# The inverse transform's second and third width groups, one row later each, in a fused window-attention and Fourier kernel

## The chip, the core and the metric

The kernel runs on one core of a Trainium2 chip. The core has a matrix engine (PE, with its own unit PEld for loading weights), a vector engine (DVE), an activation engine (ACT), a general engine (POOL) and a queue engine (SP) that issues nearly all DMAs. Each takes its instructions in order; they wait for each other through semaphores. The metric is the device time of one execution in microseconds, as the median of several runs: 3237.37 us before the change (three runs, 3235.12 to 3238.8). All arithmetic is in float32.

## What is computed

The input is 32 images of 56 x 56 tokens with 128 channels. Two residual layers follow each other, and each normalises its input over groups of 4 channels first:

```python
x = x + window_attention(group_norm(x))   # windows of 7 x 7, shifted by 3, 4 heads, relative bias, mask
x = x + feedforward(fourier(group_norm(x)))
def fourier(x):                            # for the width and for the height
    modes = dct(x)[..., :32]               # first 32 modes along that axis
    mixed = einsum('bixy,ioy->boxy', modes, w)   # a 128 x 128 matrix for each mode
    return idct(mixed, zero beyond mode 32)      # summed over both axes
def feedforward(h):
    return relu(h @ W1 + b1) @ W2 + b2     # 128 -> 512 -> 128
```

The part that the change touches is the last step of `fourier` for the width axis: the inverse transform from 32 modes back to 56 columns, which is added onto what the height axis left.

## The kernel before

The work is cut into *cycles*. In cycle r the attention works on one row of windows (7 token rows): image r // 8, attention row i = r % 8. The Fourier layer and the feed-forward of an image run behind its attention; the helper `fourier(cycle)` gives, for every cycle, the one or two images that are in that phase and their step c. An image passes steps c = 0 to 15, so two images overlap: steps c and c + 8 always share a cycle. With the attention rows they stand like this:

| attention row i | 3 | 4 | 5 | 6 | 7 | 0 | 1 | 2 |
|---|---|---|---|---|---|---|---|---|
| younger image, step c | 0 | 1 | 2 | 3 | 4 | 5 | 6 | 7 |
| older image, step c | 8 | 9 | 10 | 11 | 12 | 13 | 14 | 15 |

Below a cycle is called by its steps: "the row of 2/10" is the cycle in which one image is at step 2 and the one before it at step 10. Eight cycles, one period, take about 97 us, and 31 such periods follow each other. When the attention of the last image is over, a shorter loop body works off the rest (the tail: step 0 of the last image and everything behind it).

What the steps do, as far as the change and the prediction speak of it:

- Forward transform (`transform`, L756) for the width at step 0 and for the height at steps 1 and 2. DVE transposes the result out of a PSUM bank (`turn_modes`, L771, called from `columns_turn` at steps 1 and 2), ACT scales it (`scale_modes`, L778) and adds the mean's part (`shift_modes`, L783) into the tile `y`.
- Mixing (`mix`, L803, copied by ACT at L811): height groups at step 3, width groups at steps 4 and 5. The result `z` goes through DRAM (`zscr`) and comes back turned as the tile `zT` (`load_modes`, L824), of which there are two buffers.
- Inverse transform (`modes_back`, L842, then `fetch_back`). Each axis has four groups of 16, 16, 16 and 8 lines. A group of 16 lines is 16 matmul instructions (each is two passes, so the profile counts 32) into two banks. For the height ACT copies the banks into the tile `xf` (L865). For the width DVE adds them onto `xf` (L860), 2 instructions of 128 x 448. Which group is done at which step is told by `back_groups(c)`.
- Feed-forward at steps 8, 9, 10, 12, 13, 14 and 15 (`FF_AT`; step 11 has none): `ff_in` (L885, printed as L124, the helper `halved`) reads 512 tokens of `xf`, ACT applies bias and ReLU (L887), `ff_out` (L124 and L920) makes the output, POOL adds the second bias to the residual (L892) and DVE adds both (L930). Group 0 of `ff_in` needs the first width group, group 1 (step 9) the second, group 3 (step 12) the third, group 5 (step 14) the fourth.

In a cycle PE's order is: q and k (L124 into `pa`), `ff_in`, the attention-value product of an earlier row (L592, inside `eighths`, with `transform` behind it), the scores (L498) and the inverse transform (both in `quarters`: the scores first where the row has a feed-forward, the inverse transform first where it has none), v (L476), the mixing, `ff_out`, the projection (L637). Where the row has no feed-forward, two mixes come ahead of `eighths` and two behind v.

DVE's order in a cycle: tokens of the next image, `turn_modes` or the bank readers of `eighths` (L622), the scores' bias (L506, two), the row maximum (L516), further `turn_modes`, `last_fetch` (L860 for the steps above 8), the transpose of the probabilities (L575), the sums (L528), the reciprocal (L530), and the adds at L930 and L645. POOL subtracts the maximum (L517) and ACT takes the exponential (L523).

PSUM has eight banks: four `pa` for attention, four `pc` for the rest, each set handed out in turn. A matmul into a bank waits until its last reader is done. The order on PE, DVE, ACT and POOL is the program's; SP's is chosen by the scheduler, which issues a load as soon as its buffer can be free.

Of the kernel before, what the change touches and what calls it, by code (L numbers as in the profile page):

```python
# [50 lines left out]
def swin_fourier_kernel(  # L51
# [75 lines left out]
    def load_tokens(im, i):  # L127

        n0, n1 = WS * i // 2, WS * (i + 1) // 2
        t = xr_sb[i % 2]  # L130
        for a, e, p, src in chunks_of(x, im.b, n0, n1):
            nc.sync.dma_start(t[p, a - n0 : e - n0], src)
        im.xr[i] = t
# [11 lines left out]
    def load_quarter(b, k, u):  # L145

        if b > 1:
            t = work.tile([P, HW, KB], F32, tag="xin", name="xin", bufs=1)
        else:
            t = y_of[k][:, : S * KB].rearrange("p (w c) -> p w c", w=S)  # L150
            t = t[:, u * HW : (u + 1) * HW]
        rows = slice(k * (S - KB), k * (S - KB) + KB)
        for cb in range(C // KB):
            cs = slice(cb * KB, (cb + 1) * KB)
            queue = nc.scalar if b == 0 and cb % 2 else nc.sync
            queue.dma_start(t[cs], x[b, rows, u * HW : (u + 1) * HW, cs])
        return t
# [111 lines left out]
    def mix_weights(k):  # L269
        dst, src = ((w1sb, w1), (w0sb, w0))[k // 4]  # L270
        m = slice(k % 4 * NM // 4, (k % 4 + 1) * NM // 4)
        nc.sync.dma_start(dst[:, m], src[:, m])
# [58 lines left out]
    def image_begin(b):  # L331
        im = Image()
        im.b = b
        im.half, im.xw, im.xr, im.eT = {}, {}, {}, {}
        return im
# [3 lines left out]
    def turn_quarter(im, k, u):  # L339

        slot = WS * ROWS[k]
        if u == 0:
            im.half[k] = big.tile(
                [P, NWR * WS * ROWS[1] + JP - WT], F32, tag="xw", name="xw", bufs=3
            )
            nc.vector.memset(im.half[k][:, NWR * slot : NWR * slot + JP - WT], 0.0)
        slots = im.half[k][:, : NWR * slot].rearrange("p (j h s) -> p s j h", j=NWR, s=WS)
        slots = slots[:, :, :, :KB]
        xin = xins.pop((im.b, k, u)).rearrange("p (m s) c -> p s m c", s=WS)
        m0, m1 = u * NP, (u + 1) * NP  # L350
        nc.vector.transpose(slots[:, : WS - SS, m0:m1], xin[:, SS:])
        if u == 0:
            nc.vector.transpose(slots[:, WS - SS :, NWR - 1], xin[:, :SS, 0])
            nc.vector.transpose(slots[:, WS - SS :, : NP - 1], xin[:, :SS, 1:])
        else:
            nc.vector.transpose(slots[:, WS - SS :, m0 - 1 : m1 - 1], xin[:, :SS])
        im.first = (SS * WS, WS * WS)
        windows = im.half[k][:, : NWR * slot].rearrange("p (j t) -> p j t", j=NWR)
        for i in range(NP):
            t0 = im.first[k] + i * WT  # L360
            im.xw[NP * k + i] = windows[:, :, t0 : t0 + WT]

    def copy_wrap(im, copy):
        a, b = (
            t[:, : NWR * WS * n].rearrange("p (j h s) -> p j h s", j=NWR, s=WS)
            for t, n in zip((im.half[0], im.half[1]), ROWS)
        )
        copy(b[:, :, KB:], a[:, :, :SS])

    def row_stats(im, i):  # L370
        if i == 0:
            im.st = small.tile([P, NWR, 6], F32, tag="st0", name="st0", bufs=2)
        nc.vector.bn_stats(im.st[:, i], im.xw[i])
# [392 lines left out]
    def turn_modes(im, width, h, r):  # L766

        p = im.py[width, h][r]
        t = work.tile([P, 4, C], F32, tag="z", name="modes", bufs=4)
        t = t.rearrange("p k c -> p (k c)")[:, : 2 * CH * KB]  # L770
        nc.vector.transpose(t, p[:, : 2 * CH * KB])  # L771
        im.modes.setdefault((width, h), []).append(t)
# [78 lines left out]
    def fetch_back(im, width, g):  # L851

        l0, n = LINES[g]
        nch = n // 4
        px = im.px.pop((width, g))
        for li in range(2):
            src = px[li][:, : nch * 2 * S]
            if width:
                dst = im.xf[:, l0 : l0 + n].rearrange("p (c l r) w -> p l c (r w)", l=2, r=2)
                nc.vector.tensor_tensor(  # L860
                    dst[:, li], src.rearrange("p (c m) -> p c m", c=nch), dst[:, li], ALU.add
                )
            else:
                dst = im.xf[:, :, l0 : l0 + n].rearrange("p h (c l r) -> p l c h r", l=2, r=2)
                nc.scalar.copy(dst[:, li], src.rearrange("p (c h r) -> p c h r", c=nch, r=2))  # L865
# [98 lines left out]
    def row(r):  # L964
        return (images[r // NWR], r % NWR) if 0 <= r < NB * NWR else (None, 0)

    def fourier(cycle):

        b, c = divmod(cycle - CONV_BEGIN, NWR)
        return [(images[b - k], c + k * NWR) for k in (1, 0) if 0 <= b - k < NB]  # L970

    def back_groups(c):

        if c in (5, 6, 7):
            return [(c == 7, (c + 1) % 2 * 2 + j) for j in range(2)]
        return [(True, c // 2 - 3)] if c in (10, 12) else []

    def load_back(cycle):
        for im, c in fourier(cycle):
# [134 lines left out]

    def last_fetch(cycle):
        for im, c in fourier(cycle):
            if c > 8:
                for width, g in back_groups(c):
                    fetch_back(im, width, g)

    def columns_turn(cycle, r):
        for im, c in fourier(cycle):
            if c in (1, 2):
                turn_modes(im, False, c - 1, r)
# [154 lines left out]
    with tc.manual_schedule(engines={ET.PE, ET.Activation, ET.DVE, ET.Pool}):  # L1279
        with tc.manual_schedule(engines={ET.SP}):  # L1280
            images[0] = image_begin(0)
            for k in range(2):
                for u in range(2):
                    turn_quarter(images[0], k, u)
                if k:
                    copy_wrap(images[0], nc.vector.tensor_copy)
                for u in range(2):
                    xins[1, k, u] = load_quarter(1, k, u)
                for i in range(NP * k, NP * k + NP):
                    row_stats(images[0], i)  # L1290
            for i in range(2):
                load_tokens(images[0], i)
            for m in range(8):
                mix_weights(m)
            for _ in range(3):
                norm_step(-1)
            for r, t in ((0, 0), (0, 1), (1, 0)):
                for half in range(2):
                    bias_and_mask(nc.vector, r, t, half)
            extra = big.tile([P, S, S], F32, tag="xf", name="a_extra", bufs=2)  # L1300
            extra = extra.rearrange("p r w -> p (r w)")[:, : AT + JP - WT]
            nc.gpsimd.memset(extra[:, AT:], 0.0)
            a_ends.append(extra)
            a_sb.append(extra[:, :AT].rearrange("p (t w j) -> p t w j", t=NH, w=NP))
            for cycle in range(CONV_BEGIN):
                first_rows(cycle)
        for cycle in range(CONV_BEGIN, NB * NWR + CONV_BEGIN + FF_AT[-1] - NWR + 1):
            halves_first(cycle)
            if not row(cycle - 3)[0]:
                eighths(cycle)  # L1310
                for r in range(2):
                    columns_turn(cycle, r)
                behind_max(cycle)
                half_columns(cycle)
                half_columns(cycle, True)
                scale_first(cycle, 0)
                scale_first(cycle, 1)
                load_first(cycle)
                last_out(cycle)
                quarters(cycle)  # L1320
                last_fetch(cycle)
                load_back(cycle + 1)
                continue
            if not has_ff(cycle):
                half_columns(cycle)
            eighths(cycle)
            early = any(c == 10 for _, c in fourier(cycle))
            if early:
                columns_turn(cycle, 0)
            quarters(cycle)  # L1330
            if row(cycle)[0]:
                attn_max(cycle)
            if not early:
                columns_turn(cycle, 0)
            columns_turn(cycle, 1)
            last_fetch(cycle)
            if row(cycle)[0] and cycle % NWR in LATE_SQUARES:
                sum_squares(*row(cycle - 4))
                next_tokens(cycle)
            behind_max(cycle)  # L1340
            load_first(cycle)
            halves_last(cycle)
# [62 lines left out]
```

## Time and profile before

| what | value |
|---|---|
| median of three runs | 3237.37 us (3235.12 to 3238.8) |
| the profiled execution's own time | 3239.0 us |
| its span, first to last instruction | 3236.4 us |
| mean granted PE clock | 0.993 |
| one period of 8 cycles, mean of 22 in the middle | 97.1 us |
| its rows, i = 0 to 7 | 15.65, 10.09, 10.12, 13.39, 12.68, 13.20, 8.28, 13.67 us |
| PE busy, first 150 us | 93.97 us |
| PE busy, 600 to 3000 us | 597 to 598 of each 600 us |
| PE busy, the last 107 us | 98.64 us |

The profiled execution stands 1.6 us above the median of the runs. Its span is 2.6 us shorter than its own time. A timeline line reads: start, duration, engine, line, operation, out<-in, shape and count, and in brackets the engine's idle time ahead of it and what ended that. A matmul's end is modelled, so what PE does is best read from the starts.

### The profile page before, as it was taken

What the parts mean: (1) busy time and instruction counts of PE and PEld (TensorE: products, weight loads), DVE (VectorE), ACT (ScalarE), POOL (GpSimd) and SP (SyncE); (2) the same over time, 40 slices, a digit from 0 to 9 for tenths busy, and PEclk for the clock granted to TensorE, in tenths of its full rate; (3) what the DMA queues carried; (4) which work ended last, traced back from release to release, by engine and by line L of the source; (5) the groups of instructions that cost most, each with busy time, mean ns of one, the idle gap of its engine ahead of it and who ended that gap; (6) DMA issues with size and microseconds to landing.
All of it is one profiled execution on the core that took longest, in us unless ns stands there. A gap on an engine that the chain in (4) does not pass through costs nothing.

```text
span 3236.4 us, 151985 instructions
## 1 busy us (share of the span) xinstructions
PE 3148.4 (97%) x65664; PEld 2348.9 (73%) x65664; DVE 2516.3 (78%) x4751; ACT 2183.5 (67%) x4004; POOL 2294.3 (71%) x2570
## 2 busy tenths in 40 slices
PE   5789999999999999999999999999999999999999
PEld 4567777777777777777777777777777777777776
DVE  7678888888888888887888888878888888888741
ACT  4566776666776676776676777666776666776663
POOL 5467777777777777777777777777777777777741
PEclk9899999999999999999999999999999999999999
DMA  6446566655556665556666656556666556665453
GB/s 128 98 118 147 139 139 148 138 147 147 139 137 148 138 148 144 140 138 147 138 147 145 141 138 147 138 142 150 141 139 146 138 144 148 141 140 142 117 145 89
DMA packets 1171652, 448.47 MB, mean 139 GB/s; under 512 B 527690, under 2 KB 1141116, under 8 KB 1170980
## 3 DMA queue, kind: packets, MB, share of 16 engines
q1 hardware_dynamic: 1162788, 437.41, 57.0%
q8 instruction: 514, 8.42, 1.2%
q10 hardware_dynamic: 7584, 1.18, 0.3%
q14 instruction: 158, 1.29, 0.1%
q0 software_dynamic: 608, 0.17, 0.0%
HBM read 277.00 MB, written 161.48 MB: 135 GB/s over the span
## 4 chain that ended last, share of the span: by engine, by line
PE 50%; DMA 0%; issue 0%; ACT 0%; DVE 0%; SPq 0%; DVEq 0%; ACTq 0%
PE pc L124 23%; PE pa L124 5%; PE pa L476 4%; PE pc L803 4%; PE pa L498 3%; PE pa L637 3%; PE pa L592 3%; PE pc L842 3%; PE pc L756 2%; PE pc L920 0%; DMA zT<-zscr 0%; ACT hid L887 0%; PE pa L703 0%; DMA out_dram<-res 0%; ACT xf L865 0%
## 5 line engine op out<-in xcount | busy, mean ns | idle before, releaser
L547 POOL TENSOR_TENSOR blocks<-a,rs 32x272 f32<-32x272 f32 (+3 forms) x1434 | 1217.4, 856 | 389.2 <-DVE rs L530 271.6
L124 PE MATMUL pc<-wff,hid 128*64 128x128 f32 x12288 | 714.0, 273 | 2.4 <-ACT hid L887 1.2
L124 PE MATMUL pc<-xf,wff 128*64 128x512 f32 (+2 forms) x3584 | 714.1, 539 | 1.3 <-DVE xf L860 1.3
L124 PEld LDWEIGHTS pc<-wff,hid 128*64 128x64 f32 x12288 | 680.0, 137 | 12.2 <-ACT hid L887 6.0
L517 POOL TENSOR_TENSOR a<-a,mx 128x784 f32<-128x784 f32 x250 | 376.3, 1505 | 297.7 <-DVE mx L516 270.8
L124 PEld LDWEIGHTS pc<-xf,wff 128*64 128x64 f32 x3584 | 263.1, 136 | 372.5 <-issue 292.7
L887 ACT ACTIVATE hid<-pc,b1sb 128x512 f32<-128x512 f32 (+2 forms) x896 | 499.8, 641 | 41.6 <-PE pc L124 41.0
L124 PE MATMUL pa<-xw,wn 128*64 128x392 f32 x2048 | 393.1, 499 | 28.6 <-ACT wn L429 27.9
L506 DVE TENSOR_TENSOR a<-pa,bm 128x392 f32<-128x392 f32 x500 | 259.0, 560 | 166.0 <-PE pa L498 153.7
L483 ACT COPY v<-pa 128x512 f32<-128x512 f32 x256 | 151.9, 593 | 286.0 <-PE pa L476 283.4
L463 ACT ACTIVATE k<-pa,bqkv,heads 128x392 f32<-128x392 f32 x512 | 318.5, 673 | 15.5 <-ACT q L450 1.1
L138 POOL TENSOR_TENSOR xr<-xr,bproj 128x384 f32<-128x384 f32 (+1 forms) x256 | 292.4, 1142 | 44.7 <-DMA xr<-in_x_dram 22.4
L892 POOL TENSOR_TENSOR res<-res,b2sb 128x512 f32<-128x512 f32 (+1 forms) x224 | 251.7, 1124 | 87.4 <-DMA res<-scr 70.0
L778 ACT ACTIVATE y<-modes,rstd 128x448 f32<-128x448 f32 x256 | 276.8, 1140 | 42.4 <-DVE modes L771 31.8
L450 ACT ACTIVATE q<-pa,bqkv 128x392 f32<-128x392 f32 x256 | 149.6, 585 | 227.5 <-PE pa L124 225.6
L523 ACT ACTIVATE a<-a 128x784 f32<-128x784 f32 x250 | 214.0, 856 | 130.9 <-POOL a L517 130.5
L575 DVE STREAM_TRANSPOSE eT<-blocks 128x1024 f32<-128x1024 f32 x240 | 295.3, 1230 | 0.0
L592 PEld LDWEIGHTS pa<-eT,v 49*32 49x32 f32 x16384 | 173.0, 106 | 158.7 <-issue 69.7
L476 PE MATMUL pa<-wn,xw 128*64 128x128 f32 x4096 | 281.5, 279 | 1.6 <-issue 1.2
L528 DVE TENSOR_REDUCE sm<-a 128x16 f32<-128x784 f32 x250 | 239.9, 959 | 53.5 <-ACT a L523 53.4
L516 DVE TENSOR_REDUCE mx<-a 128x16 f32<-128x784 f32 x250 | 242.2, 969 | 7.6
L476 PEld LDWEIGHTS pa<-wn,xw 128*64 128x64 f32 x4096 | 219.7, 137 | 36.5 <-issue 2.4
(126 smaller groups left out, 4980.4 us busy)
## 6 DMA issues: line engine op xcount, KB each, us to landing
zscr<-z SPq DMA_DIRECT2D x512, 112.0 KB
xin<-in_x_dram SPq DMA_DIRECT2D x480, 112.0 KB
htok<-scr SPq DMA_DIRECT2D x128, 392.0 KB
zT<-zscr SPq DMA_DIRECT2D x192, 256.0 KB
res<-scr SPq DMA_DIRECT2D x160, 256.0 KB
out_dram<-res SPq DMA_DIRECT2D x160, 256.0 KB
scr<-x SPq DMA_DIRECT2D x256, 112.0 KB
xr<-in_x_dram SPq DMA_DIRECT2D x256, 84.0 KB
```

The source lines that it names most:

```text
L124: nc.tensor.matmul(dst[ps], lhsT=lhsT[:, ps], rhs=rhs, start=start, stop=stop)
L138: nc.gpsimd.tensor_tensor(piece, piece, bproj.unsqueeze(1).to_broadcast([P, n, C]), ALU.add)
L463: nc.scalar.activation(k_sb[:, u], pk[:, :RT].rearrange("p (w j) -> p w j", j=WT), AF.Identity, bias=im.bias[:, 3 + u : 4 + u], scale=head ...
L476: nc.tensor.matmul(pv[HALVES[w % 2], w // 2 * C : (w // 2 + 1) * C], lhsT=im.half[i // NP][:, t0 : t0 + JP], rhs=im.w[:, 2 * C : 3 * C], s ...
L506: nc.vector.tensor_tensor(a[:, 2 * hp : 2 * hp + 2, :, 0:WT].rearrange("p u w j -> p w u j"), ps[hp][:, :RT].rearrange("p (w u j) -> p w u ...
L517: nc.gpsimd.tensor_tensor(a3, a3, mx.unsqueeze(2).to_broadcast([P, 2 * NWR, WT]), ALU.subtract)
L547: nc.gpsimd.tensor_tensor(dst[to, k, :, :n], a3[src, :, kb * KB : kb * KB + n], rs[src].unsqueeze(2).to_broadcast([src.stop - src.start, 2 ...
L575: nc.vector.transpose(eT.rearrange("p t (k j) -> p k t j", k=2), blocks[r % 2])
L592: nc.tensor.matmul(po4[u][h * HD : (h + 1) * HD, pr], lhsT=v[ks, pr, h * HD : (h + 1) * HD], rhs=eT[ks, h * NP + pr, :WT], start=True, sto ...
L778: nc.scalar.mul(y[:, r], t.rearrange("p (n k) -> p n k", k=NM), im.rstd)
L887: nc.scalar.activation(hf[:, :n], ph[:, :n], AF.Relu, bias=b1sb[:, f : f + 1])
L892: nc.gpsimd.tensor_tensor(im.res[:, :k], im.res[:, :k], b2sb.unsqueeze(1).to_broadcast([P, k, C]), ALU.add,)
```

## The change

The first width group stays at step 7 and the fourth at step 12. The second moves from step 7 to step 8, the third from step 10 to step 11. `last_fetch`, which adds a width group behind the row maximum, now takes step 8 in as well. The special order of the row of 2/10, in which the first `turn_modes` of step 2 stood ahead of the scores, is gone: both `turn_modes` of that row now come behind the row maximum.

```diff
     def back_groups(c):
-        if c in (5, 6, 7):
-            return [(c == 7, (c + 1) % 2 * 2 + j) for j in range(2)]
-        return [(True, c // 2 - 3)] if c in (10, 12) else []
+        if c in (5, 6):
+            return [(False, 2 * (c - 5) + j) for j in range(2)]
+        width_at = (7, 8, 11, 12)
+        return [(True, width_at.index(c))] if c in width_at else []
...
     def last_fetch(cycle):
         for im, c in fourier(cycle):
-            if c > 8:
+            if c >= 8:
                 for width, g in back_groups(c):
                     fetch_back(im, width, g)
...
             eighths(cycle)
-            early = any(c == 10 for _, c in fourier(cycle))
-            if early:
-                columns_turn(cycle, 0)
             quarters(cycle)
             if row(cycle)[0]:
                 attn_max(cycle)
-            if not early:
-                columns_turn(cycle, 0)
+            columns_turn(cycle, 0)
             columns_turn(cycle, 1)
             last_fetch(cycle)
```

No operation is added or taken away; the number of instructions of each kind is the same.

## The prediction

> **What bounds the kernel now.** I read the page first, then the stretches, PE's waits, and the timelines of PE, DVE, ACT and POOL over one period.
>
> ```profile
> span 3236.4 us, 151985 instructions
> PE 3148.4 (97%) x65664; PEld 2348.9 (73%) x65664; DVE 2516.3 (78%) x4751; ACT 2183.5 (67%) x4004; POOL 2294.3 (71%) x2570
> ...
> 231.00:3100.00 2869.00, 2856.79 (x59706) 2131.70 (x59704) 2321.27 (x4345) 2003.20 (x3667) 2149.59 (x2396) 1.00 0.60 142
> ...
> PE pc L842 <- issue: 8.5, 10, 1.2
> ```
>
> From 231 to 3100 us PE idles for 12.2 of 2869 us. Most of it, 8.5 us, lies in the inverse transform (L842) and was ended by no other engine. So moving PE work from row to row is worth nothing in itself; what counts is which waits vanish and which appear. The stall looks like this:
>
> ```profile
> 2055.94 1.60 PE L842 MATMUL pc<-idctw,zT 64*64 64x112 f32 x57
> 2058.59 0.42 PE L842 MATMUL pc<-idctw,zT 64*64 64x112 f32 x7 [1.05 <-issue]
> ```
>
> Between two matmuls of one group, with nothing to wait for, PE stops 1.05 us. Counting PE's instructions along the trace, these stalls lie at one place modulo 256 (194 to 196), and the page's instruction queue moved 8.42 MB in 514 packets, 16 KB each, which is 256 PE instructions a packet: PE waits for its own program. Counting also what the modelled ends hide, the 28 periods in the middle lose 15.5 us so: 7.6 in the row of 7/15, 5.7 in 5/13, 1.6 in 0/8, 0.7 in 4/12.
>
> **The change, part by part.**
>
> *The moved matmuls.* One group of 16 lines is 16 instructions. What it takes of PE is the distance from the scores to v with it, in the row of 2/10, less that without, in 1/9:
>
> ```profile
> 1693.44 0.89 PE L498 MATMUL pa<-k,q 64*49 64x98 f32 x32
> 1694.26 1.09 PE L476 MATMUL pa<-wn,xw 128*64 128x128 f32 x16
> ...
> 1706.09 0.89 PE L498 MATMUL pa<-k,q 64*49 64x98 f32 x32
> 1706.80 0.94 PE L842 MATMUL pc<-idctw,zT 64*64 64x112 f32 x32
> 1707.68 1.09 PE L476 MATMUL pa<-wn,xw 128*64 128x128 f32 x16
> ```
>
> 1.59 - 0.82 = 0.77 us. The rows of 7/15 and 2/10 lose 0.77 us each, those of 0/8 and 3/11 gain it: zero in sum, but PE reaches what follows 2/10 earlier.
>
> *The adds onto xf* (L860, two, 1.12 us) move along on DVE. In 0/8 they stand between maximum and transpose; DVE idles 0.91 us before the sums there, and the rest of 0.2 us meets POOL's 1.09 us of idle time before L547. In 3/11 they delay DVE by 1.12 us; the idle 1.54 us before the next L506 (1727.56) takes it, and `ff_in` of step 12 (1722.37) needs the adds done, which happens at 1719.70 + 1.12 = 1720.8. No cost; without that cover up to 1.1 us a period. In 0/8 the second group takes the two banks that `turn_modes` reads first, free at 1680.42 + 1.13 = 1681.55, while PE is there at 1681.83, both 0.77 earlier now: 0.28 us to spare. In 7/15, DVE's chain to the statistics matmul (L703), which today ends within 0.08 us of PE in half of the periods, gets 1.1 us shorter while PE gets 0.77 shorter: worth 0.03 us a period. The first 231 us are DVE's; there the same shortening gives some 0.3 us. I set both against POOL's rstd (L421), which gets tight (0 to 0.1 us late by my count of the divisions before it): nothing together.
>
> *The loads.* SP issues a zT load when its buffer frees: two together at 1671.67 (1.46 us for the pair) become one in 7/15 and one in 0/8. Behind the first stands the load of htok (1679.41), 0.73 us later, whose data is needed at 1692.4. They are used 15 us later or more. No cost; with the cover gone, 0.73 us a period.
>
> *The removed special order*, with PE 0.77 us earlier, bears on step 3. The first mix waits for ACT's last step on y:
>
> ```profile
> 1707.01 1.04 DVE L506 TENSOR_TENSOR a<-pa,bm 128x392 f32<-128x392 f32 x2
> 1708.09 0.97 DVE L516 TENSOR_REDUCE mx<-a 128x16 f32<-128x784 f32 x1
> 1708.97 0.64 DVE L771 STREAM_TRANSPOSE modes<-pc 128x448 f32<-128x448 f32 x1
> ...
> 1709.30 1.16 ACT L778 ACTIVATE y<-modes,rstd 128x448 f32<-128x448 f32 x1
> 1710.67 0.86 ACT L523 ACTIVATE a<-a 128x784 f32<-128x784 f32 x1 [0.21 <-POOL a L517]
> 1711.43 1.15 ACT L778 ACTIVATE y<-modes,rstd 128x448 f32<-128x448 f32 x1
> 1712.61 0.34 ACT L783 ACTIVATE y<-y,shift 128x56 f32<-128x56 f32 x1
> ...
> 1714.08 1.91 PE L803 MATMUL pc<-w1sb,y 128*64 128x128 f32 x32
> ```
>
> Today y is ready at 1712.95, 1.13 us ahead. Now the first turn ends only at 1708.97 + 0.64 = 1709.61; ACT's first scaling starts about 1709.65 and ends at 1710.81; the exponential, queued behind it, starts 0.14 us late, and so do the second scaling and the shift, and PE behind them. Margin: 1.13 - 0.77 - 0.14 = 0.22 us, of which the semaphore takes 0.05. So most periods don't wait. But in 11 of 28 periods today's margin is under 0.91 us (down to 0.08), because DVE there is late behind xin (DVE waits 57.2 us for that DMA in all). The sum of 0.96 less each margin, where positive, is 4.6 us over 28 periods, 0.16 us a period. Against it: in 0/8 DVE now frees xin's buffer some 0.5 us earlier, and if the DMA gains that, 0.03 is left. I take 0.08, in the middle: 29 x 0.08 = 2.4 us (0.9 to 4.6).
>
> *PE's program fetch.* A stall needs 256 instructions in a short time. In 7/15 the dense run is values, scores, two groups: 128 + 64 + 128 instructions in some 3.0 us; it loses 64, and v and `ff_out` (0.03 us an instruction) follow sooner. From how the stall falls with time in hand I keep 0.04 of its 0.27 us a period: -6.7 us. In 0/8 the run gains 64, but the transform in it is slow (1.7 us for 64): +2. In 3/11 a new run arises: values 128, group 64, scores 64 in 0.74 + 0.77 + 0.82 = 2.3 us, as dense as 7/15 was, though it follows the mixing, not `ff_in`: 0.16 us a period, +4.7. The program is also 3 instructions a period shorter (fewer waits apart), which spreads where the packets end: +1.4 in the rows of 5/13 and 4/12. Sum +1.4 us. Bounds: the 7.6 us of 7/15 gone and nothing new, -7.6; 3/11 as bad as 7/15 and 0/8 as 3/11 is estimated, with 7/15 halved, +9. I take the middle, since the rows share one cause.
>
> The Trainium skill (Runtime: NRT & Kernel Launch, section Instruction fetch mechanics) says that each engine streams its program in blocks of 256 instructions, and that crossing a block is mostly hidden. The trace agrees on the block and shows the crossing at up to 1.05 us here; by the rule the term would be 0 and the sum 1.4 us lower.
>
> *The tail.* With no attention left, a width group straight ahead of the `ff_in` that reads it shows its DVE add:
>
> ```profile
> 3145.83 1.00 PE L842 MATMUL pc<-idctw,zT 64*64 64x112 f32 x32
> 3146.76 3.71 PE L803 MATMUL pc<-w1sb,y 128*64 128x128 f32 x64
> ...
> 3206.23 1.00 PE L842 MATMUL pc<-idctw,zT 64*64 64x112 f32 x32
> 3208.54 3.65 PE L124 MATMUL pc<-xf,wff 128*64 128x512 f32 x16 [1.31 <-DVE xf L860]
> ```
>
> Hidden, a group costs 0.93 us (followed by the mixing); exposed, 2.31. In the built order the second-last image has group two right ahead of `ff_in` of step 9: 2.31 - 0.77 = +1.54. Its group three now comes behind the mixes, ahead of `ff_in` of step 12: +1.38. The last image: step 7 goes from 2.91 (3181.18 to 3184.09, with a wait for the second zT) to 2.31, -0.60; step 8 gains a whole group, +2.31. Sum 4.63, less 0.29 us of a zT wait (3176.81) that 2.9 us of delay cover: +4.3 (3 to 5).
>
> **Sum:** 2.4 + 1.4 + 4.3 = +8.1 us on the profiled 3239.0 us, so 3247.1; this execution is 1.6 above the median, hence 3245.5 us, 0.25% slower. The likeliest case's own range: 0.9 - 1 + 3 to 4.6 + 4 + 5, 3240 to 3251.
>
> **The rivals.**
>
> *A. Nothing that can be measured* (0.2% is 6.5 us, what a measurement here can tell from none). The fetch term comes out at -3 and xin's gain leaves 0.9 us: 4.3 + 0.9 - 3 = +2.2, 3239.6 us. For it: two terms nearly cancel by my own count. Chance 0.25.
>
> *B. Faster.* The change breaks up the dense runs, and the new ends of the packets miss those in 5/13 too: the whole 15.5 us go. -15.5 + 4.3 + 2.4 = -8.8, 3228.6 us. For it: all the idle time that PE has in the periods is of this kind. Against it: 5/13 isn't touched and 3/11 gets denser. It decides from 11 of the 15.5 us on, where with 4.3 us of tail the gain passes 6.5. Chance 0.13.
>
> *C. The mix waits in every period.* If the exponential or the scaling slips by another 0.5 us (ACT has four steps in a row there, and POOL's L517 feeds one), each period pays 0.3 to 0.5: 29 x 0.4 = 11.6, + 4.3 + 1.4 = +17.3, 3254.7 us. For it: the margin is 0.17 us by two differences. Against it: POOL's part doesn't move. Chance 0.15.
>
> **How the numbers follow.** The forecast has 0.47. Slower: 0.47 + 0.15 = 0.62; same 0.25; faster 0.13. The time is the forecast's, 3245.5. The range for 8 in 10 takes in A, most of C and the upper half of B: 3230 to 3255.
>
> **What would show it.** Right: in the row of 2/10 v comes 0.77 us nearer to the scores; waits "PE pc L803 <- ACT y L783" appear at step 3, some 2 us in all; issue stalls leave 7/15 and appear in 3/11; the tail shows three waits of some 1.3 us on "DVE xf L860" in place of one. Wrong: issue stalls under 5 us in all, L803 waiting in nearly every period, or a wait on L429 or L842's banks that I set at nothing.

## The result, and the profile after

The changed kernel takes 3257.2 us (median of six runs, 3252.01 to 3258.77) against 3237.07 us beside it: 1.0062 times as long, 95% interval 1.0052 to 1.0072, or 20.1 us. Predicted were 3245.5 us: the direction was right, the size was not, and the time lies above the range of 3230 to 3255 us. One execution of e7, an experiment below, took 4550.28 us at a granted clock of 0.654; e7's ratio leaves it out, and its median, 3242.59 us, would be 3242.47 us without it. These are the page, the stretch of the periods, and PE's waits in that stretch; the prediction shows the same lines of before:

```profile
span 3254.7 us, 151784 instructions
PE 3155.0 (97%) x65664; PEld 2354.2 (72%) x65664; DVE 2533.3 (78%) x4751; ACT 2178.8 (67%) x4004; POOL 2296.7 (71%) x2570
```

```profile
231.00:3100.00 2869.00, 2849.36 (x59402) 2125.02 (x59398) 2330.29 (x4331) 1990.02 (x3649) 2139.15 (x2381) 1.00 0.59 141
```

The waits of after, from 231 to 3100 us (total, number, longest):

```profile
PE pa L124 <- ACT wn L429: 8.8, 23, 0.9
PE pc L842 <- issue: 6.2, 8, 1.3
PE pa L476 <- issue: 2.3, 6, 0.5
PE pc L124 <- issue: 1.0, 2, 0.7
PE pc L803 <- issue: 0.5, 2, 0.3
```

The granted clock is the same (0.993), and in the same 2869 us PE gets through 304 matmul records fewer and is busy 7.4 us less. The first line is new: q of the next image (L124 into `pa`) waits for `wn`, the weights scaled by that image's norm (L429), 23 times in some 29 periods. The prediction named this wait among the things that would make it wrong. The list counts from modelled matmul ends, which hide a part; the starts of the rows show all of it. Means of 22 periods in the middle, in us, by attention row i (steps below):

| | i=0 | 1 | 2 | 3 | 4 | 5 | 6 | 7 |
|---|---|---|---|---|---|---|---|---|
| steps | 5/13 | 6/14 | 7/15 | 0/8 | 1/9 | 2/10 | 3/11 | 4/12 |
| before | 15.65 | 10.09 | 10.12 | 13.39 | 12.68 | 13.20 | 8.28 | 13.67 |
| after | 15.53 | 10.13 | 9.05 | 14.37 | 12.71 | 12.46 | 9.10 | 14.10 |

The moved groups are seen as 0.75 to 1.07 us off the rows of 7/15 and 2/10 and 0.82 to 0.98 us on 0/8 and 3/11. What is left over is the row of 4/12, +0.43 us, in which no matmul was moved.

These are, in one period of after, the scores' bias and the third group's adds (L860) in the row of 3/11, the sums behind them, and the end of the row of 4/12, out of the timelines of DVE, POOL, ACT and PE:

```profile
1822.67 1.04 DVE L506 TENSOR_TENSOR a<-pa,bm 128x392 f32<-128x392 f32 x2 [2.74 <-PE pa L498]
...
1824.63 1.15 DVE L860 TENSOR_TENSOR xf<-pc,xf 128x448 f32<-128x448 f32 x2
...
1829.88 0.95 DVE L528 TENSOR_REDUCE sm<-a 128x16 f32<-128x784 f32 x1
1830.87 0.25 DVE L530 RECIPROCAL rs<-sm 128x16 f32<-128x16 f32 x1
...
1832.57 1.04 DVE L506 TENSOR_TENSOR a<-pa,bm 128x392 f32<-128x392 f32 x2 [0.90 <-PE pa L498]
...
1835.99 0.68 DVE L405 TENSOR_TENSOR turned<-turned 128x32 f32<-128x32 f32 x1
1836.70 0.19 DVE L386 TENSOR_REDUCE gsums<-turned 128x8 f32<-128x32 f32 x1
1836.92 1.32 DVE L389 TENSOR_SCALAR gmeans<-gsums 128x32 f32<-128x32 f32 x1
...
1838.62 0.15 DVE L417 SCALAR_TENSOR_TENSOR ve<-back 128x1 f32<-128x1 f32 x1
...
1831.27 5.35 POOL L547 TENSOR_TENSOR blocks<-a,rs 128x512 f32<-128x512 f32 x6 [1.34 <-ACT hid L887]
1836.70 1.50 POOL L517 TENSOR_TENSOR a<-a,mx 128x784 f32<-128x784 f32 x1
1838.85 0.55 POOL L421 TENSOR_TENSOR rstd<-ve,mhalf 128x1 f32<-128x1 f32 x1 [0.65 <-DVE ve L417]
...
1839.44 0.61 ACT L429 ACTIVATE wn<-wqkv,rstd 128x384 f32<-128x384 f32 x1 [3.07 <-POOL rstd L421]
...
1840.10 0.88 PE L124 MATMUL pa<-xw,wn 128*64 128x392 f32 x4 [0.27 <-ACT wn L429]
```

And the same in before, which the prediction had not shown:

```profile
1814.48 1.04 DVE L506 TENSOR_TENSOR a<-pa,bm 128x392 f32<-128x392 f32 x2 [2.19 <-PE pa L498]
...
1820.71 0.96 DVE L528 TENSOR_REDUCE sm<-a 128x16 f32<-128x784 f32 x1
1821.70 0.25 DVE L530 RECIPROCAL rs<-sm 128x16 f32<-128x16 f32 x1
...
1824.38 1.04 DVE L506 TENSOR_TENSOR a<-pa,bm 128x392 f32<-128x392 f32 x2 [1.89 <-PE pa L498]
...
1827.75 1.38 DVE L405 TENSOR_TENSOR turned<-turned 128x32 f32<-128x32 f32 x1
1829.16 0.19 DVE L386 TENSOR_REDUCE gsums<-turned 128x8 f32<-128x32 f32 x1
1829.38 0.18 DVE L389 TENSOR_SCALAR gmeans<-gsums 128x32 f32<-128x32 f32 x1
...
1829.95 0.15 DVE L417 SCALAR_TENSOR_TENSOR ve<-back 128x1 f32<-128x1 f32 x1
...
1822.10 5.35 POOL L547 TENSOR_TENSOR blocks<-a,rs 128x512 f32<-128x512 f32 x6 [1.34 <-DVE rs L530]
1827.52 1.56 POOL L517 TENSOR_TENSOR a<-a,mx 128x784 f32<-128x784 f32 x1
1830.18 0.55 POOL L421 TENSOR_TENSOR rstd<-ve,mhalf 128x1 f32<-128x1 f32 x1 [1.10 <-DVE ve L417]
...
1830.76 0.62 ACT L429 ACTIVATE wn<-wqkv,rstd 128x384 f32<-128x384 f32 x1 [2.58 <-POOL rstd L421]
...
1831.48 0.83 PE L124 MATMUL pa<-xw,wn 128*64 128x392 f32 x4
```

Read them from the scores' bias on (L506). The two L506 stand 9.90 us apart in both kernels, but the sums L528 begin 6.23 us behind the first of them before and 7.21 us after, since on DVE they come behind the third group's adds. POOL's division L547 needs the sums' reciprocal L530; it began 2.28 us ahead of the second L506 before and 1.30 us ahead after, 0.15 us behind the end of L530 in both (the line of after names ACT's L887 as what ended POOL's idle time, but the reciprocal is what moved). So POOL's subtraction L517 ends at 4.70 us after L506 before and at 5.63 after. DVE meanwhile works through the next image's norm, small steps of 0.15 to 0.25 us, but one of them lasts 1.38 us (L405) or 1.32 us (L389), and it ends 0.04 to 0.05 us after L517 does. In all 22 periods of either profile just one of L404, L405 and L389 is stretched so, to 1.15 to 1.53 us, and ends 35 to 50 ns after L517. In after it is L389 each time; in 20 of them L405 is held too, for 0.57 to 0.68 us, until the last of the six divisions ends. The Trainium skill (SBUF — State Buffer, section Who interferes with whom) says that POOL's SBUF ports are a pair that it shares with DVE, that a DVE instruction with two inputs in SBUF contends with a POOL instruction that reads SBUF, that a `tensor_scalar` in a mode with two ports contends too and then whoever issues first keeps the pair for the whole instruction, and that a `tensor_reduce` never contends on this chip. The durations agree: L404 and L405 have two inputs in SBUF, L389 is a `tensor_scalar`, and the reduction L386 keeps its 0.19 us. That the ports are the cause, and which mode L389 runs in, no run here shows by itself; that the step stands still beside L517 and not without it, e5 below shows.

So the end of L517 sets `ve`, `rstd`, `wn` and q. It comes 0.91 us later after L506 (means of 22: 4.74 and 5.65 us). Fewer small steps are left behind it (0.57 us instead of 0.98), so `ve` is 0.50 us later, and 0.1 us of room that `wn` had on average is used up: q is 0.41 us later.

### The profile page after: what moved, and what is told of

It is laid out like the page before. It is cut to its first block, busy times and chain, and to the rows that moved or that the text cites. A ratio compares the mean times of both kernels' runs of the same rounds, so it can differ in the third digit from the quotient of the medians.

```text
span 3254.7 us, 151784 instructions
## 1 busy us (share of the span) xinstructions
PE 3155.0 (97%) x65664; PEld 2354.2 (72%) x65664; DVE 2533.3 (78%) x4751; ACT 2178.8 (67%) x4004; POOL 2296.7 (71%) x2570
## 5 line engine op out<-in xcount | busy, mean ns | idle before, releaser
L547 POOL TENSOR_TENSOR blocks<-a,rs 32x272 f32<-32x272 f32 (+3 forms) x1434 | 1219.0, 857 | 388.9 <-DVE rs L530 227.7
L124 PE MATMUL pc<-xf,wff 128*64 128x512 f32 (+2 forms) x3584 | 715.2, 539 | 6.8 <-DVE xf L860 6.6
L124 PE MATMUL pc<-wff,hid 128*64 128x128 f32 x12288 | 713.6, 273 | 2.5 <-issue 1.0
L124 PEld LDWEIGHTS pc<-wff,hid 128*64 128x64 f32 x12288 | 680.0, 137 | 12.3 <-ACT hid L887 6.0
L517 POOL TENSOR_TENSOR a<-a,mx 128x784 f32<-128x784 f32 x250 | 376.3, 1505 | 274.3 <-DVE mx L516 245.5
L124 PEld LDWEIGHTS pc<-xf,wff 128*64 128x64 f32 x3584 | 266.7, 136 | 374.8 <-issue 296.3
L887 ACT ACTIVATE hid<-pc,b1sb 128x512 f32<-128x512 f32 (+2 forms) x896 | 500.8, 643 | 48.3 <-PE pc L124 47.8
L124 PE MATMUL pa<-xw,wn 128*64 128x392 f32 x2048 | 393.6, 498 | 37.1 <-ACT wn L429 36.7
L506 DVE TENSOR_TENSOR a<-pa,bm 128x392 f32<-128x392 f32 x500 | 259.1, 560 | 189.6 <-PE pa L498 177.5
L476 PE MATMUL pa<-wn,xw 128*64 128x128 f32 x4096 | 283.7, 279 | 3.2 <-issue 2.3
L528 DVE TENSOR_REDUCE sm<-a 128x16 f32<-128x784 f32 x250 | 239.2, 957 | 29.7 <-ACT a L523 29.6
L476 PEld LDWEIGHTS pa<-wn,xw 128*64 128x64 f32 x4096 | 220.8, 137 | 38.7 <-issue 3.8
```

The source lines that it names most:

```text
L124: nc.tensor.matmul(dst[ps], lhsT=lhsT[:, ps], rhs=rhs, start=start, stop=stop)
L476: nc.tensor.matmul(pv[HALVES[w % 2], w // 2 * C : (w // 2 + 1) * C], lhsT=im.half[i // NP][:, t0 : t0 + JP], rhs=im.w[:, 2 * C : 3 * C], s ...
L506: nc.vector.tensor_tensor(a[:, 2 * hp : 2 * hp + 2, :, 0:WT].rearrange("p u w j -> p w u j"), ps[hp][:, :RT].rearrange("p (w u j) -> p w u ...
L517: nc.gpsimd.tensor_tensor(a3, a3, mx.unsqueeze(2).to_broadcast([P, 2 * NWR, WT]), ALU.subtract)
L547: nc.gpsimd.tensor_tensor(dst[to, k, :, :n], a3[src, :, kb * KB : kb * KB + n], rs[src].unsqueeze(2).to_broadcast([src.stop - src.start, 2 ...
L887: nc.scalar.activation(hf[:, :n], ph[:, :n], AF.Relu, bias=b1sb[:, f : f + 1])
```

## The experiments

Two theories stood against each other. L, the late divide, is the chain above. M holds the moved matmuls themselves responsible, wherever they stand. In each comparison before ran beside the kernel on the same chip; its medians were 3234.8 (e1 to e4), 3233.4 (e5, e6, e8, e9), 3238.5 (e7, after_again) and 3234.0 us (the last two).

**One group at a time.** e1 moves the second group alone, e2 the third:

In e1, against before (the special order of 2/10 stays):

```diff
-        if c in (5, 6, 7):
-            return [(c == 7, (c + 1) % 2 * 2 + j) for j in range(2)]
-        return [(True, c // 2 - 3)] if c in (10, 12) else []
+        if c in (5, 6):
+            return [(False, 2 * (c - 5) + j) for j in range(2)]
+        width_at = (7, 8, 10, 12)
+        return [(True, width_at.index(c))] if c in width_at else []
...
-            if c > 8:
+            if c >= 8:
```

In e2, against after (without that order):

```diff
-        if c in (5, 6):
-            return [(False, 2 * (c - 5) + j) for j in range(2)]
-        width_at = (7, 8, 11, 12)
-        return [(True, width_at.index(c))] if c in width_at else []
+        if c in (5, 6, 7):
+            return [(c == 7, (c + 1) % 2 * 2 + j) for j in range(2)]
+        return [(True, c - 9 if c == 11 else 3)] if c in (11, 12) else []
...
-            if c >= 8:
+            if c > 8:
```

> The kernel before with the second width group alone moved (step 7 to 8). Theory L (late divide): the loss per period is the third group's adds, which in the row of 3/11 delay DVE's sums, POOL's division and its subtraction L517, so that rstd and wn for the next image come 0.4 us late at the end of the row of 4/12. Then this kernel has no wait of PE on ACT wn L429 (under 1 us in all), the row of 4/12 stays at 13.67 us, and only the second group's share of the tail is paid (1.54 - 0.60 + 2.31 - 0.29 = 3.0 us), less 0 to 3 us of issue stalls that leave the row of 7/15: 3237 to 3240 us. Rival M (moved matmuls): the loss comes of PE's groups standing elsewhere, whichever group it is, and the adds cost nothing: half of the 10 us per run is paid here, 3245 us or more.

> The kernel before with the third width group alone moved (step 10 to 11), the special order of the row of 2/10 gone as in the change. Theory L: the whole wait on wn is here: row of 4/12 at 14.1 us instead of 13.67, 29 x 0.43 = 12.5 us, and 1.4 us of the tail: 3251 us (3248 to 3254). Rival M: half of the loss, 3243 to 3246 us, the row of 4/12 under 13.9 us.

e1: 3236.44 us, 1.0007 (0.9998 to 1.0016) of before; no wait on L429 in the list, row of 4/12 at 13.66 us, and 2.1 us more from the start of the last attention row to SP's last issue (157.0 us against 154.9; the tail's length is taken so below). e2: 3252.36 us, 1.0052 (1.0039 to 1.0064); row of 4/12 at 14.09 us, and this line in its waits:

```profile
PE pa L124 <- ACT wn L429: 8.8, 24, 1.0
```

The loss per period is the third group's alone, so M falls: the second group's matmuls cost the periods nothing. Whether the third group's matmuls or its adds cost them, these two runs can't tell; the next one does.

**The adds without the matmuls.** e4 is before with two reductions on DVE where the change puts the adds:

```diff
             last_fetch(cycle)
+            if row(cycle)[0] and cycle % NWR == 6:
+                for k in range(2):
+                    junk = small.tile([P, 1], F32, tag="junk", name="junk", bufs=2)
+                    nc.vector.tensor_reduce(junk, wff1, axis=AX.X, op=ALU.add)
```

> The kernel before, nothing moved; in the row of 3/11 DVE does two added reductions (128x512 of a constant tile into an unused one, about 1.2 us together) at the place where the change puts the third group's adds. They are work that the reference doesn't need. Theory L: wn late as after the change, row of 4/12 14.0 to 14.2 us, the run 10 to 13 us longer: 3247 to 3251 us. Rival M: DVE has the room, 3235 to 3239 us.

Measured: 3252.02 us, 1.0051 (1.0038 to 1.0064). The row of 4/12 takes 14.23 us, and the wait is there with no matmul moved:

```profile
PE pa L124 <- ACT wn L429: 11.9, 28, 0.9
```

```profile
1825.73 1.27 DVE L1340 TENSOR_REDUCE junk<-wff 128x1 f32<-128x512 f32 x2
```

The two reductions take 1.27 us, L517 ends 1.08 us later against L506 than in before (means of 22 periods), and the row grows by 0.56 us. Time on DVE at this place is enough to make the loss.

**The divide back where it was.** e3 is after, with the norm's first steps behind the sums in the row of 4/12:

```diff
-        if cycle % NWR == NWR - 1:
-            norm_step(cycle)
         tokens_bias(cycle)
...
             divide(cycle)
+        if cycle % NWR == NWR - 1:
+            norm_step(cycle)
```

> The kernel after; in the row of 4/12 the four first DVE instructions of the next image's norm (L397, L400, L386, L389, 1.0 us together) are put behind the sums and reciprocal (L528, L530), so POOL's division starts about 1.0 us earlier, where it was before the change; no matmul moves. Theory L: wn is back in time, the row of 4/12 back at 13.67 us, the run 12.5 us shorter: 3244.7 us (3242 to 3248). Rival M: nothing, 3255 to 3259 us.

Measured: 3244.56 us, 1.0030 (1.0018 to 1.0041). The lines of the same period of e3:

```profile
1826.52 1.04 DVE L506 TENSOR_TENSOR a<-pa,bm 128x392 f32<-128x392 f32 x2 [0.80 <-PE pa L498]
...
1824.04 5.36 POOL L547 TENSOR_TENSOR blocks<-a,rs 128x512 f32<-128x512 f32 x6 [0.33 <-ACT hid L887]
1829.47 1.50 POOL L517 TENSOR_TENSOR a<-a,mx 128x784 f32<-128x784 f32 x1
...
1833.61 0.83 PE L124 MATMUL pa<-xw,wn 128*64 128x392 f32 x4
```

The division is back at 2.48 us ahead of L506, q waits for nothing, and the row of 4/12 is at 13.67 us again. Against before the loss shrinks from 20.1 to 9.8 us. Of these the tail explains 3.3; this version moves the groups as after does and keeps after's tail.

**The subtraction out of the way.** e5 leaves the divide late and puts POOL's L517 behind L421 in the row of 4/12:

```diff
         nc.vector.tensor_reduce(mx, a3, axis=AX.X, op=ALU.max)
+        if r < CONV_BEGIN or r % NWR != NWR - 1:
+            attn_less_max(r)
+
+    def attn_less_max(r):
...
         nc.gpsimd.tensor_tensor(
             a3, a3, mx.unsqueeze(2).to_broadcast([P, 2 * NWR, WT]), ALU.subtract
...
         if cycle % NWR == NWR - 1:
             norm_step(cycle)
+            if cycle in maxima:
+                attn_less_max(cycle)
```

> The kernel after; in the row of 4/12 POOL's subtraction of the maximum (L517) is put behind the rstd of the next image (L421). Division, adds and all PE work stay where the change has them. Theory P (the last step of theory L): one DVE instruction of the norm (L404, L405 or L389) stands still until POOL's L517 ends, so it is the end of L517 that sets rstd. With L517 behind it, rstd comes about 1.1 us earlier although the division is as late as after the change; the wait on wn is gone, the row of 4/12 back at 13.67 us, 3244 to 3248 us. Rival Q (the late division itself, or a DVE that is slow beside any POOL work, holds rstd): the row stays at 14.0 us or more, 3254 to 3259 us.

Measured: 3245.66 us, 1.0042 (1.0029 to 1.0055). In its timeline (line numbers stand 8 higher below the edit) L389 is down to 0.18 us and `rstd` comes ahead of the subtraction:

```profile
1827.24 1.04 DVE L506 TENSOR_TENSOR a<-pa,bm 128x392 f32<-128x392 f32 x2 [0.97 <-PE pa L498]
...
1831.54 0.18 DVE L389 TENSOR_SCALAR gmeans<-gsums 128x32 f32<-128x32 f32 x1
...
1825.88 5.36 POOL L555 TENSOR_TENSOR blocks<-a,rs 128x512 f32<-128x512 f32 x6 [1.34 <-ACT hid L895]
1832.40 0.55 POOL L421 TENSOR_TENSOR rstd<-ve,mhalf 128x1 f32<-128x1 f32 x1 [1.16 <-DVE ve L417]
1832.92 1.50 POOL L525 TENSOR_TENSOR a<-a,mx 128x784 f32<-128x784 f32 x1
```

The division starts 1.36 us ahead of L506, as late as in after, and still `rstd` begins 5.16 us after L506 instead of 6.28; the row of 4/12 is at 13.65 us, and `wn` has 0.68 us to spare on average. In after POOL was idle for 0.65 us ahead of L421, waiting for DVE, so there it was DVE's step and not POOL's own queue that came last. So it is the standing still behind L517, and not the late division by itself, that costs, and rival Q falls. The run is still 12.3 us above before. Its tail is 3.5 to 4.1 us longer than before's; its issue stalls are 15.0 us by the count below, 11.1 of them in the row of 0/8, more than in any other kernel here, but in sum they lie between those of before's two profiles. So a part of the 12.3 us stays open.

**The tail.** e6 is after with the last two images at the steps of before:

```diff
-        width_at = (7, 8, 11, 12)
-        return [(True, width_at.index(c))] if c in width_at else []
+        width_at = (7, 8, 11, 12) if im.b < NB - 2 else (7, 7, 10, 12)
+        return [(True, g) for g in range(4) if width_at[g] == c]
```

> The kernel after, with the width groups of the last two images at the steps of before (7, 7, 10, 12); the 30 images ahead as the change has them. By the prediction's tail term 4.3 us less (3 to 5): 3253 us, and the stretch from the last attention row to the end 3.3 us shorter, as the two traces differ there. Rival: the tail's waits are covered by what follows and the stretch differs by run only: 3256 to 3258 us.

Measured: 3248.7 us, 1.0046 (1.0034 to 1.0059), 15.3 us above before. The tail takes 152.8 us; after took 158.2, before 154.9. PE's waits from that row on, after and then before:

```profile
PE pc L124 <- DVE xf L860: 6.6, 5, 1.4
```

```profile
PE pc L124 <- DVE xf L860: 1.3, 1, 1.3
PE pc L842 <- DMA zT<-zscr: 1.3, 2, 1.0
```

Five exposed adds stand in place of one. In return the waits for zT are gone; they are gone in e6 too, which is 1.3 of the 2.1 us by which e6's tail is shorter than before's. Why the loads there are in time with the tail's own steps unchanged was not tried.

**The special order.** e8 is after with the first `turn_modes` of 2/10 ahead of the scores again:

```diff
+            early = any(c == 10 for _, c in fourier(cycle))
+            if early:
+                columns_turn(cycle, 0)
             quarters(cycle)
...
-            columns_turn(cycle, 0)
+            if not early:
+                columns_turn(cycle, 0)
             columns_turn(cycle, 1)
```

> The kernel after, with the special order of the row of 2/10 put back (first transpose of the modes ahead of the scores). The prediction put 2.4 us (0.9 to 4.6) on its removal through ACT's last step on y (L783); the trace of after shows that step 0.35 us ahead of PE in every period, so by that nothing is gained: row of 2/10 at 12.46 us and row of 3/11 at 9.10 us as after, 3255 to 3259 us. By the prediction's term 2.4 us less, 3254.8 us.

Measured: 3254.18 us, 1.0064 (1.0052 to 1.0077); rows of 2/10 and 3/11 at 12.46 and 9.09 us. Against before this is the loss of after, so the removed order is worth nothing that can be measured here.

**The second group, but not in the tail.** e9 is e1 with the tail of before (as in e6).

> The kernel before with the second width group at step 8 for the first 30 images only; the last two as before. By the runs so far: e1's middle (rows 32 to 248, 2615.4 us against 2618.8 before) without its tail (157.0 against 154.9): 3 to 5 us less than before, 3230 to 3232 us on the chip where before gave 3234.8. If the issue stalls in the rows of 7/15 only moved to other rows, as much as before.

Measured: 3233.85 us, 1.0000 (0.9991 to 1.0009). The gain that one profile of each had promised is not there: the miss is before's first profile, which held more issue stalls than its second (below). No version here beats before.

**Both repairs.** e7 is e3 with e6's tail; it and both kernels were run once more.

> The kernel after with both repairs: the norm's first DVE steps behind the sums (as in e3) and the last two images at the steps of before (as in e6). If the late wn and the tail are all that the change costs, what is left is before within its noise: e3's stretch of rows 32 to 248 (2618.2 us, before 2618.8) with e6's tail (152.8 us, before 154.9), a ratio to before of 0.999 to 1.002. Rival: the change costs something else as well, at the start or in the issue stalls, as e3's median (9.8 us above before, where its tail explains 3.3) might say: a ratio of 1.002 or more.

> The kernel after unchanged, for the same chip as e7 and for a second look at the start (first Fourier row at 125.4 us after, 123.4 before, though both run the same instructions up to there). If the 2 us at the start belong to the run and not to the kernel, that row starts anywhere in 122.6 to 125.4 us, as in the other profiles. The middle (2631.8 us) and the tail (158.2 us) repeat within 1 us; the ratio to before is 1.0052 to 1.0072.

> The kernel before unchanged, for a second profile of it on the chip of e7_again. If the start belongs to the run, the first Fourier row and row 32 stand elsewhere than in the first profile (123.4 and 376.4 us) by up to 2 us, while rows 32 to 248 (2618.8 us), the issue stalls (16.0 us) and the row of 4/12 (13.67 us) repeat within 1.5 us.

> e7 once more: its median stood 4.1 us above before, its one profile 1.6 us below. If the profile fell on a quick run, this one shows where the 4 us lie: in the start (row 32 later than 376.4 us by 2 to 4) or in the issue stalls (rows 32 to 248 at 2620 to 2623 us). If the median was chance, the ratio comes out at 1.0005 or less.

e7 gave 3242.59 us, 1.0014 (1.0005 to 1.0023), and again 3239.0 us, 1.0016 (1.0007 to 1.0025); after_again 3260.62 us, 1.0075 (1.0061 to 1.0089), slightly above what was expected; before_again 3233.39 us, 0.9999 (0.9990 to 1.0008). On one chip the two repairs give back 18.0 us (3260.62 - 3242.59) of 22.1. The first Fourier row begins at 122.5 to 125.4 us over all profiles, so what the start differs by belongs to the run. The middle and the stalls did not repeat as closely for before as was expected. By the count of the prediction (stops over 0.15 us near one place modulo 256, 30 periods, us):

| | all | 5/13 | 7/15 | 0/8 | 3/11 | images 29, 30 | rows 32 to 248 |
|---|---|---|---|---|---|---|---|
| before | 16.0 | 6.0 | 7.6 | 1.6 | 0 | 0 | 2618.8 |
| before_again | 11.2 | 4.9 | 5.3 | 0.7 | 0 | 0 | 2613.4 |
| after | 15.4 | 4.7 | 0.3 | 7.7 | 1.2 | 3.6 | 2631.8 |
| after_again | 16.7 | 5.4 | 0.4 | 9.3 | 0.6 | 4.4 | 2632.6 |
| e7 | 15.8 | 6.8 | 0 | 7.4 | 0.9 | 4.9 | 2620.4 |
| e7_again | 15.0 | 3.6 | 0 | 8.6 | 1.0 | 3.3 | 2618.2 |
| e9 | 12.1 | 1.8 | 0 | 5.7 | 0 | 0 | 2615.2 |

What e7 keeps of the loss, 4 to 5 us, is of the size of its stalls in images 29 and 30 (3.3 to 4.9 us), which neither profile of before has; but all its stalls together are no more than those of before's first profile, and its profiles end only 2.5 us after before_again's. So where these microseconds lie is not shown. One of the new stalls of after, in the row of 0/8:

```profile
2368.13 0.75 PE L842 MATMUL pc<-idctw,zT 64*64 64x112 f32 x23
2370.16 0.44 PE L842 MATMUL pc<-idctw,zT 64*64 64x112 f32 x9 [1.28 <-issue]
```

## Why the prediction was right in direction and wrong in size

Of the loss of 20.1 to 22.1 us only the tail, 3.3 to 3.9 us, is shown to come by a mechanism that the prediction had priced. Where the step that failed is repaired (e3), the change is 9.8 us slower, so the sign did not hang on luck alone; that this number lies near the forecast's 8.1 us is luck, since 2.4 us of the forecast are a wait that did not come.

**The moved matmuls: right.** v comes 0.83 us after the scores in the row of 2/10 instead of 1.59 (1712.24 and 1713.07 below), so 0.76 us nearer; forecast were 0.77 us.

**The adds: wrong, and this is the step that failed.** The prediction set the third group's adds at "no cost", since DVE has 1.54 us idle before the next L506, and POOL's `rstd` at "0 to 0.1 us late". DVE does absorb them: its idle time there falls from 1.89 to 0.90 us. But the sums L528 lie between the adds and that idle time, and POOL hangs on the sums, not on L506. In the divisions the prediction counted only a delay of 0 to 0.1 us for `rstd`, and it has no term for a step of DVE's norm that stands still until L517 ends. That lay open in the timeline of before (the 1.38 us of L405, a step of 0.19 us elsewhere), and I had not read it. It costs 0.43 us a period, 29 x 0.43 = 12.5 us, where I had nothing. By the row of 4/12 alone, summed over 29 periods, it is 13.1 us (396.6 to 409.7), and e3 is back at 396.6.

**The mix at step 3: wrong, 2.4 us too much.** These are the lines of after that answer to those of the prediction:

```profile
1712.24 0.89 PE L498 MATMUL pa<-k,q 64*49 64x98 f32 x32
1713.07 1.09 PE L476 MATMUL pa<-wn,xw 128*64 128x128 f32 x16
...
1719.47 1.92 PE L803 MATMUL pc<-w1sb,y 128*64 128x128 f32 x32
...
1715.13 1.17 DVE L771 STREAM_TRANSPOSE modes<-pc 128x448 f32<-128x448 f32 x2
...
1718.76 0.34 ACT L783 ACTIVATE y<-y,shift 128x56 f32<-128x56 f32 x1
```

y is ready at 1719.10, 0.37 us ahead of PE; 0.35 to 0.38 us in all 22 periods, where I had put 0.17 to 0.22 us and shortfalls in 11 of 28. No period shows the late DVE that I had counted in 11 of before. The profiles of the experiments show what freed it: the second group's move. y is less than 0.91 us ahead of PE in 2 of 28 periods of e1 and in 1 of e9 (images 2 to 29), which move that group and leave the order of 2/10 as it was, but in 10 of before, 9 of before_again and 14 of e4, which do not move it; and in the row of 2/10 DVE stands idle ahead of L351, which needs the load of xin, for 30.8 and 29.5 us in the former, 43.2, 38.0 and 46.5 us in the latter. That agrees with the prediction's case that DVE frees xin's buffer earlier and the load gains it; the way from the one to the other was not followed. The low end of the term (0.9) was nearer. In e2, which moves the third group alone, the late DVE does cost: PE waits 2.9 us in eight periods, though ahead of v (L476) for a bank that DVE's L622 reads, and not for y. The loads, which I set at nothing, cost nothing: PE waits for no zT in the periods. Rival C, a wait in every period, came within 2.5 us of the median (3254.7 us) by luck: its wait, at the mix, occurs in no period.

**The program fetch: in sum within the noise, wrong in place.** I took -6.7 us in 7/15, +2 in 0/8, +4.7 in 3/11 and +1.4 elsewhere. The pairs of profiles show -7.3 and -4.9, +6.1 and +8.6, +1.2 and +0.6. So 7/15 was right, and the dense run did not go to 3/11 but to 0/8, where the second group now stands. All stalls together went from 13.6 to 16.1 us as means of two profiles, +2.5; forecast +1.4. Two profiles of one kernel differ by up to 4.8 us, so neither the sum nor its sign is shown. Rival B is refuted: the stalls change places and stay.

**The tail: right.** 154.9 to 158.2 us, or 154.3 to 158.2: +3.3 and +3.9; forecast 4.3 (3 to 5). Among the signs I named three exposed adds; there are five, as many as the sum itself has (four new ones and the one of before).

With the measured sizes the sum is 12.5 + 3.6 + 2.5 = 18.6 us, against 20.1 and 22.1 us in the medians; 1.5 to 3.5 us are not assigned.

## What to carry to other kernels

Idle time further down an engine's queue covers inserted work only if nothing between the two is read by another engine; so follow each result behind the insertion to its reader, and from there to the engine that bounds the kernel. An instruction that shows two durations in one trace can hide a wait that no list of waits shows: find what ends at the same moment, and put the short instruction ahead of the long one that holds it. Before calling a difference of a few microseconds a gain, take the profile of the same kernel twice.

## What the hardware showed unexpectedly

A DVE step of 0.18 us stood for up to 1.53 us beside one POOL instruction of 1.5 us, in every period, and ended 35 to 50 ns after it; as soon as POOL was idle, the same step took 0.18 us (e5). And PE's issue stalls are not a fixed tax: the same program lost 16.0 us to them in one run and 11.2 us in another, and e7 has them in images where before has none (3.3 to 4.9 us in images 29 and 30).
